# A third accumulator bank in turn, the second batch's first norm in two passes, and a wider spread feed-forward tail in a two-layer transformer kernel

## Chip, cores and metric

The kernel runs on one core of a Trainium2 chip. The metric is the device time of one execution in microseconds. Engines: PE does the matmuls and writes to PSUM, which has eight banks; DVE, ACT and POOL do element-wise work, and POOL doesn't read PSUM here; SP issues every DMA of the program, one after the other. PEld is the weight load ahead of a matmul.

## What is computed

The input x is (2, 1024, 256) in float32. Two layers follow, each attention and then a feed-forward part, and each part is wrapped in a norm before and a norm after ("sandwich"):

```
x = x + ln(attn0(ln(x)))   # 16 heads of 128, weights as FP4 codes x scales, softmax over all 1024 keys
x = x + ln(ffn0(ln(x)))    # silu(gate) * up -> down, ternary weights, inner width 704
x = x + ln(attn1(ln(x)))   # 16 heads of 16, causal
x = x + ln(moe(ln(x)))     # 2 shared + 16 routed experts of 128, top 8 by sigmoid, all computed and weighted

def _layernorm(x, eps=1e-05):
    m = jnp.mean(x, -1, keepdims=True); v = jnp.var(x, -1, keepdims=True)
    return (x - m) / jnp.sqrt(v + eps)
```

## The kernel before

**Numbers.** Activations are split in a high and a low 16-bit part, and products are sums of two or three 16-bit matmuls. So most results that leave PSUM pass ACT (bias, cast to the high part) and then DVE or POOL (the low part, by a subtraction).

**Steps.** `l0_attn` walks through 256 steps, one for each query tile (128 rows) of a head of layer 0. A step issues the scores of its tile (`l0_soft`, into a `pss` buffer), the split of the tile before (`l0_split`, whose transpose goes through SP as `PT`), the product with v for a tile some steps back (`l0_av`, into `psa`), and the jobs that are due: weights of the next pair of heads (`l0_dequant`, into `psy`), q, k and v of the next head (`l0_qk`, `l0_v`, into `psp`), the output product (`l0_out`). Other work is put into steps by `at(step, [functions], spacing)`, with constants at the top of the file: staging of later weights (`PRE`, `FFN_W`), batch 1's first norm (`LN_B`, from step 101), batch 0's feed-forward (`FFN_AT`, steps 120 and 144), its layer-1 q, k, v (`QKV_AT`, 136 and 160) and its layer-1 attention (from step 149), batch 1's first feed-forward half (`FFN1_AT`, 246).

**Tail.** After step 255 a planner in `run` orders what is left against a made-up clock t: `on(t, functions, spacing, cost)` makes work due, `C_FFN`, `C_QKV`, `C_X3`, `C_ROUTE` say when. What is left is the second feed-forward half of batch 1, its layer-1 attention, and nearly all of the experts: 144 units of 12 matmuls (L1233), each followed some units later by its down product of 6 (L1264).

**Order.** PE's order is as the program issues it. The order on DVE, ACT, POOL and SP is made by a list scheduler at build time, from priorities; each engine then works strictly in that order, and an instruction that waits holds up all behind it.

**PSUM.** `pss` has two buffers of two banks; `psp` two of one bank; `psa` and `psy` one bank each. `new_ps` hands out a bank for feed-forward and expert units: `psp`, or in turn with `pss` where layer-1 attention doesn't use it (`l1_over`). The other products take `psp` directly. `psy` serves the dequantization (the last one in step 95) and later the sums of layer-1 attention (`av` in `l1_attn`, L1042).

**Norms.** `stats` (L119, L120) takes mean and variance of two row tiles, `rstd` (L100 to L110) a reciprocal root by eight small dependent DVE instructions on 128x2 values; L147 normalizes, `split` casts on ACT (L219) and subtracts on POOL (L220), and an SP transpose stores the result as `xa` or `xb`. `ln_load` loads two row tiles into `y` (three buffers), normalizes and transposes them; `ln_add` does the norm after a part, the addition, and the next norm.

**Layer-1 q and k.** `l1_qkv.qk` computes 512 columns, `scaled` makes both halves in the tile `l1_sq` (L503 and L506 on ACT, L507 on POOL), three DMAs store it to DRAM (L916) and two load it back in the layout of the attention (L921). For batch 0 `l1_sq` has one buffer (tag `hl_w`); for batch 1 it takes a buffer of the tag `e`, which has three, one of them held by expert weights to the end.

Of the kernel before, what the change touches and what calls it, by code (L numbers as in the profile page):

```python
# [9 lines left out]
F32 = mybir.dt.float32  # L10
# [4 lines left out]
ALU = mybir.AluOpType  # L15
# [32 lines left out]
PAD = 480  # L48
# [8 lines left out]
FFN_W = 102  # L57
LN_B = (101, 105, 103, 106, 115, 120, 117, 121)
# [16 lines left out]
C_FFN = (18.21, 2.02)  # L75
# [3 lines left out]
C_ROUTE = (9.53, 8.0, 30.0, 12.0)  # L79
# [6 lines left out]
class Net:  # L86
# [6 lines left out]
    def rstd(self, var, eps, w):  # L93
# [14 lines left out]
        y = sp.tile([P, NT], F32, name="rs_y")[:, :n]  # L108
# [71 lines left out]

    def ln_start(self, xs):
# [109 lines left out]
    def setup(self, ctx):  # L291
# [19 lines left out]
        self.l1_over = False  # L311
# [95 lines left out]
    def l0_dequant(self, dst, codes, sc, n):  # L407
# [6 lines left out]
        nc.vector.tensor_mul(dst, codes, ps.rearrange("p (k f) -> p k f", k=2))  # L414

# [48 lines left out]
    def l0_qk(self, st, which, c):  # L464
# [6 lines left out]
        ps = self.psp.tile([P, 512], F32, name="psp")  # L471
# [37 lines left out]
    def l0_v(self, st, t4):  # L509
# [4 lines left out]
        ps = self.psp.tile([P, 512], F32, name="psp")  # L514
# [95 lines left out]
    def l0_out(self, st, t2):  # L610
# [6 lines left out]
        ps = self.psp.tile([P, 512], F32, name="psp")  # L617
# [169 lines left out]
    def ffn(self, b, half):  # L787
# [29 lines left out]
        def down(c):  # L817
            ps = self.psp.tile([P, 512], F32, name="psp")
# [58 lines left out]
    def l1_kd(self):  # L877
# [9 lines left out]
        self.n_kd = 0  # L887

    def l1_qkv(self, b, m):
# [4 lines left out]
        def qk(which, c):  # L894
            n = "qk"[which]
            sq = p.tile([P, 2, 512], F16, name="l1_sq", tag=("hl_w", "e")[b], bufs=(1, 3)[b])
# [6 lines left out]
            ps = self.psp.tile([P, 512], F32, name="psp")  # L903
# [29 lines left out]
        def vv(t4):  # L933
# [3 lines left out]
            ps = self.psp.tile([P, 512], F32, name="psp")  # L937
# [18 lines left out]
    def l1_attn(self, b, m, st, yT):  # L956
# [212 lines left out]
    def moe(self, b):  # L1169
# [55 lines left out]
        def unit(c, e):  # L1225
# [15 lines left out]
            nc.vector.scalar_tensor_tensor(th, pu, 1.0 / 16, th, op0=ALU.mult, op1=ALU.mult)  # L1241
# [64 lines left out]
    def run(self):  # L1306
        nc, tc = self.nc, self.tc
        with ExitStack() as ctx:
# [240 lines left out]
```

## Time and profile before

| | us |
|---|---|
| runs: 1808.83, 1806.64, 1804.91; median | 1806.64 |
| the profiled execution's own time | 1804.53 |
| its span, first to last instruction | 1802.8 |
| PE busy (matmuls), DVE, ACT, POOL | 1610.4, 1270.7, 1111.1, 897.7 |
| mean granted PE clock | 0.972 |

The span in stretches. Steps 101 to 121 lie at 405 to 505 us, steps 122 to 158 at 505 to 726 us, step 255 at 1251 us.

| stretch, us | PE busy | DVE busy | ACT busy | POOL busy | granted clock |
|---|---|---|---|---|---|
| 0 to 45 | 22.9 | 25.1 | 21.3 | 17.4 | 1.00 |
| 45 to 405 | 354.1 | 240.5 | 285.3 | 231.5 | 1.00 |
| 405 to 505 | 79.1 | 87.7 | 62.6 | 67.2 | 0.91 |
| 505 to 730 | 190.8 | 169.3 | 139.5 | 127.8 | 0.95 |
| 730 to 1260 | 483.8 | 382.0 | 380.6 | 260.1 | 0.99 |
| 1260 to 1530 | 220.3 | 188.8 | 99.1 | 91.2 | 0.92 |
| 1530 to 1803 | 259.4 | 177.3 | 122.6 | 102.5 | 0.98 |

A row of the timeline reads: start, duration, engine, line, operation, out<-in, shapes, and in brackets the engine's idle time just before and what ended it. PE's busy time counts a matmul longer where the clock is halved, so a busy PE isn't PE at full speed.

### The profile page before, as it was taken

The page shows a single profiled execution, that of the slowest core. Times are in us where ns is not written, and L with a number is a line of the kernel's source. Part 1 is how long each engine was busy: PE and PEld are TensorE (multiplying, and loading weights), DVE is VectorE, ACT ScalarE, POOL GpSimd, SP SyncE. Part 2 cuts the span into 40 slices and gives each one's busy share as a digit, 9 for nine tenths or more (in the row PEclk, how much of TensorE's full clock was granted, in tenths as well). Part 3 has the DMA queues.
Part 4 walks back from the last instruction along what each step waited for, and adds up shares of the span by engine and source line. Part 5 has one row for each costly group of instructions (what it writes and reads, how often), then busy time and mean ns, then how long its engine had stood idle before and what let it go on. Part 6 is the DMA issues. An engine that isn't in the chain of part 4 may idle for free.

```text
span 1802.8 us, 35972 instructions
## 1 busy us (share of the span) xinstructions
PE 1610.4 (89%) x13903; PEld 1074.9 (60%) x13903; DVE 1270.7 (70%) x2559; ACT 1111.1 (62%) x1856; POOL 897.7 (50%) x701
## 2 busy tenths in 40 slices
PE   5999999998789879999989889889867898999998
PEld 2566666665456555565555555555645575777777
DVE  5666666667988769665877677886858578765666
ACT  4788788777566655678667667677333443555432
POOL 3666667556765644445444434475433233333443
PEclk9999999999999999999999999999989899999999
DMA  5886887989966874596566667796753222111120
GB/s 124 205 185 163 170 182 176 230 194 207 243 152 150 152 130 103 107 163 140 132 161 168 190 176 163 184 209 158 238 134 99 75 74 66 46 35 54 59 71 13
DMA packets 634228, 256.19 MB, mean 142 GB/s; under 512 B 574852, under 2 KB 614568, under 8 KB 633800
## 3 DMA queue, kind: packets, MB, share of 16 engines
q1 hardware_dynamic: 634056, 253.88, 60.4%
q8 instruction: 109, 1.79, 0.4%
q14 instruction: 63, 0.52, 0.1%
HBM read 75.61 MB, written 35.33 MB: 62 GB/s over the span
## 4 chain that ended last, share of the span: by engine, by line
PE 48%; DVE 22%; ACT 10%; DMA 8%; issue 6%; POOL 2%; SPq 2%; ACTq 0%; DVEq 0%; POOLq 0%
PE pss L561 10%; PE psa L603 9%; PE psp L1233 7%; DVE nm L565 4%; DVE l_nm L982 3%; PE psp L474 3%; ACT e L567 3%; PE psa L1264 3%; PE psy L1050 3%; ACT hl L575 2%; DMA pre_ew<-hl_w 2%; PE psp L621 2%; SPq L588 2%; PE pss L1023 2%; DVE ln_st L119 1%
## 5 line engine op out<-in xcount | busy, mean ns | idle before, releaser
L576 POOL TENSOR_TENSOR hl<-e,hl 128x1024 f16<-128x1024 f32 x231 | 493.3, 2136 | 422.0 <-ACT hl L575 310.5
L561 PE MATMUL pss<-k,q 128*128 128x512 f16 x1536 | 382.9, 385 | 40.3 <-ACT e L567 10.9
L603 PE MATMUL psa<-PT,v 128*128 128x256 f16 x3072 | 410.8, 275 | 5.4 <-ACT qk L501 5.2
L565 DVE TENSOR_REDUCE nm<-pss 128x1 f32<-128x1024 f32 x256 | 312.4, 1220 | 144.8 <-PE pss L561 144.3
L567 ACT ACTIVATE e<-pss,nm 128x1024 f32<-128x1024 f32 x256 | 285.9, 1117 | 121.2 <-DVE nm L565 103.9
L603 PEld LDWEIGHTS <-v 128*128 128x128 f16 x3072 | 296.1, 99 | 99.1 <-issue 22.0
L575 ACT CAST hl<-e 128x1024 f16<-128x1024 f32 x256 | 268.7, 1050 | 4.4 <-DMA PT<-hl 1.1
L561 PEld LDWEIGHTS <-q 128*128 128x128 f16 x1536 | 146.5, 99 | 190.1 <-issue 47.2
L982 DVE TENSOR_REDUCE l_nm<-pss 128x2 f32<-128x1024 f32 (+3 forms) x152 | 176.1, 1161 | 32.7 <-PE pss L976 28.5
L1233 PEld LDWEIGHTS <-ew 128*128 128x128 f16 x1728 | 167.6, 100 | 49.5 <-issue 24.6
L1250 POOL TENSOR_TENSOR m_h<-m_t,m_h 128x256 f16<-128x256 f32 x144 | 97.3, 678 | 187.2 <-ACT m_h L1249 185.3
L474 PE MATMUL psp<-xa,wr 128*128 128x512 f16 x512 | 131.7, 380 | 13.5 <-DVE k L486 5.2
L1233 PE MATMUL psp<-xa,ew 128*128 128x256 f16 x1008 | 129.5, 280 | 7.4 <-DVE m_t L1241 2.9
L1240 DVE SCALAR_TENSOR_TENSOR m_t<-m_t,psp 128x256 f32<-128x256 f32 x119 | 49.6, 416 | 102.3 <-ACT m_t L1239 99.3
L1249 ACT CAST m_h<-m_t 128x256 f16<-128x256 f32 x144 | 58.1, 404 | 95.6 <-POOL m_t L1248 38.6
L630 DVE SCALAR_TENSOR_TENSOR acc<-psp,r,acc 128x256 f32<-128x256 f32 x240 | 104.2, 475 | 14.8 <-PE psp L621 13.9
L507 POOL TENSOR_TENSOR OT<-qk,OT 128x512 f16<-128x512 f32 x64 | 80.8, 1263 | 55.7 <-ACT OT L506 25.5
L1264 PE MATMUL psa<-ed,m_h 128*128 128x256 f16 x756 | 105.0, 276 | 0.0
L1239 ACT ACTIVATE m_t<-psp 128x256 f32<-128x256 f32 x119 | 45.6, 383 | 87.8 <-PE psp L1233 86.9
L621 PE MATMUL psp<-wo,OT 128*128 128x256 bf16 x512 | 79.5, 277 | 14.6 <-DVE ff_t L813 3.8
L1264 PEld LDWEIGHTS <-m_h 128*128 128x128 f16 x864 | 85.7, 99 | 11.1
L474 PEld LDWEIGHTS <-wr 128*128 128x128 bf16 x512 | 49.0, 98 | 69.4 <-issue 17.4
(186 smaller groups left out, 2631.2 us busy)
## 6 DMA issues: line engine op xcount, KB each, us to landing
cb<-cT_d SPq DMA_DIRECT2D x32, 512.0 KB
w_c<-in_w_codes SPq DMA_DIRECT2D x8, 1024.0 KB
x_d<-y SPq DMA_DIRECT2D x24, 256.0 KB
xr<-x_d SPq DMA_DIRECT2D x24, 256.0 KB
pre_ew<-hl_w SPq DMA_DIRECT2D x18, 256.0 KB
PT<-hl SPq DMA_TRANSPOSE x256
k_d<-k SPq DMA_DIRECT2D x8, 512.0 KB
v_d<-v SPq DMA_DIRECT2D x8, 512.0 KB
```

The source lines that it names most:

```text
L474: nc.tensor.matmul(ps, w()[:, 1 - which, kt, hs], self.xT[0, st["b"], c][:, :, 2 * j + kt, :], start=(kt == 0 and j == 0), stop=(kt == 1 a ...
L561: nc.tensor.matmul(ps[:, sl], q[:, a, qs], k[:, bb, sl], start=(a == 0 and bb == 0), stop=(a == 1), skip_group_check=True)
L565: nc.vector.reduce_max(nm, ps, axis=AX.X, negate=True)
L567: nc.scalar.activation(e, ps, AF.Exp, bias=nm, accum_out=st["sum"][:, qt : qt + 1])
L575: nc.scalar.copy(hl[:, 0, :], e)
L576: (nc.vector if lo_dve else nc.gpsimd).tensor_sub(hl[:, 1, :], e, hl[:, 0, :])
L603: nc.tensor.matmul(ps, v[:, x, kt, :], PT[:, 8 * y + kt, :], start=(kt == 0 and n == 0), stop=(kt == 7 and n == 2))
L621: nc.tensor.matmul(ps[:, 256 * i : 256 * i + 256], OT[:, j, t * P : (t + 1) * P], self.wo[st["p"], h // 2][:, h % 2, :], start=(j == 0), s ...
L630: nc.vector.scalar_tensor_tensor(ys, pv, r, ys, op0=ALU.mult, op1=ALU.add)
L982: nc.vector.reduce_max(nms[t][:, i % 2, :, j0 : j0 + nj, c], pv, axis=AX.X)
L1233: nc.tensor.matmul(ps[:, 256 * o : 256 * o + 256], self.ew[e][:, o, a, kt, :], xT[:, sl, 2 * x + kt, :], start=(n == 0), stop=(n == 5))
L1264: nc.tensor.matmul(py[:, 256 * t : 256 * t + 256], h[:, a, t * P : (t + 1) * P], self.ed[e][:, w, :], start=False, stop=(e == NE - 1 and t ...
```

## The change

1. `new_ps` gives every third request the bank `psy` while `psy_free` is set, and the products that took `psp` directly (q, k, v and output of layer 0, feed-forward down, q, k, v of layer 1) now ask `new_ps`. `psy_free` is set at step 108 if all dequantizations are done, cleared by the first layer-1 sum of a batch, and set again when batch 0's last sum has been copied out. Where `pss` is in turn, it now gets two of six requests, next to each other, and no longer every second one.
2. Batch 1's first norm is split (`ln_ahead`): its four loads and sums are placed at steps 14 to 31, with one `rstd` for all eight tiles; at the steps of `LN_B` the rows are loaded a second time (one step ahead) and only normalized.
3. In the tail the feed-forward's units start at 22.0 and are 3.0 apart on the planner's clock; the norm of the last rows ahead of batch 0's experts (`ln_load(3, 0, 4)` and `(3, 0, 6)`) comes 3.0 later, its DVE instructions behind those of the last expert unit issued; routing comes later.
4. `l1_sq` for batch 0 rotates over three buffers (one of `hl_w`, two of `st`); for batch 1 the k and the q of one column block share one buffer of `e`.
5. A padding tile shrinks by 32 bytes, which the eight kept reciprocal roots take.

The instruction counts of PE, ACT and POOL stay. DVE has 24 fewer (three `rstd` chains), SP four more loads. PE's order is the same up to the tail, but for three places where neighbouring products change sides.

```diff
 RS_S = (3.0 / 8.0) ** 0.2
 RS_START = 1593872682
 RS_NEWTON = 1.66
-PAD = 480
+PAD = 448
 L1_LEAD = 7
 SHIFT_LAG = 2
 AV_LAG = 2
...
 LN_HURRY = 580
 PRE = (12, 2.0, 186, 2.05)
 FFN_W = 102
+LN_A = 14
+PSY_AT = 108
 LN_B = (101, 105, 103, 106, 115, 120, 117, 121)
 L1_W = (100, 104)
 FFN_AT = ((120, 144), 0.55)
...
 MOE_LAG = 6
 MUL_DVE = 0.5
 C_L1 = 3.2
-C_FFN = (18.21, 2.02)
+C_FFN = (22.0, 3.0)
 C_QKV = (6.0, 14.0, 3.4)
 C_ST = (18.0, 26.0)
 C_X3 = 13.09
-C_ROUTE = (9.53, 8.0, 30.0, 12.0)
+C_ROUTE = (18.0, 16.0, 30.0, 16.0)
 C_COST = (1.9, 1.2)
 WS1 = 16.0
 SC1 = 0.5
...
         nc.vector.scalar_tensor_tensor(h, w[:, 0, :], -1.0, w[:, 1, :], op0=ALU.mult, op1=ALU.mult)
         nc.vector.scalar_tensor_tensor(w, h.unsqueeze(1).to_broadcast([P, 2, n]), RS_NEWTON, w, op0=ALU.add, op1=ALU.mult)
         nc.vector.tensor_mul(h, w[:, 0, :], w[:, 1, :])
-        y = sp.tile([P, NT], F32, name="rs_y")[:, :n]
+        y = sp.tile([P, NT], F32, name=keep or "rs_y", **(dict(bufs=1) if keep else {}))[:, :n]
         nc.vector.scalar_tensor_tensor(y, h, -10.0 / 3.0 * RS_S**2, h, op0=ALU.add, op1=ALU.mult)
         nc.vector.scalar_tensor_tensor(y, y, 5.0 * RS_S**4, w[:, 1, :], op0=ALU.add, op1=ALU.mult)
         return y
...
             x = st.pop()
             st.append(self.ln_hl(x, x))
         return [load, norm, lambda: self.ln_T(layer, b, t0, st.pop())]
+    def ln_ahead(self):
+        nc, st = self.nc, {}
+        def load(n):
+            st[n] = self.new_y()
+            with self.gate():
+                nc.sync.dma_start(st[n], self.rows(self.x[0, 1, n // 2], 2 * n % 4, 2))
+        def sums(n):
+            if n == 0:
+                st["mv"] = self.small.tile([P, NT, 2], F32, name="ln_mv8", bufs=1)
+            x = st.pop(n)
+            for i in range(2):
+                t = self.small.tile([P, 6], F32, name="ln_st")
+                nc.vector.bn_stats(t, x[:, i, :])
+                nc.vector.bn_aggr(st["mv"][:, 2 * n + i, :], t)
+            if n == 3:
+                st["r"] = self.rstd(st["mv"][:, :, 1], EPS, NT, "rs_y8")
+        def norm(n):
+            x = st.pop(n)
+            for j in range(2):
+                i = 2 * n + j
+                nc.vector.tensor_scalar(x[:, j, :], x[:, j, :], st["mv"][:, i, 0:1], st["r"][:, i : i + 1],
+                                        op0=ALU.subtract, op1=ALU.mult)
+            hl = st["hl", n] = self.work.tile([P, 4 * D], F16, name="ln_hl", bufs=2)
+            self.split(hl, x, nc.gpsimd)
+        def put(n):
+            self.ln_T(0, 1, 2 * n, st.pop(("hl", n)))
+        return ([(lambda n=n: load(n), lambda n=n: sums(n)) for n in range(4)],
+                [(lambda n=n: load(n), lambda n=n: norm(n), lambda n=n: put(n)) for n in range(4)])
     def ln_start(self, xs):
...
     def new_ps(self):
         self.n_ps += 1
-        if self.l1_over and self.n_ps % 2:
+        if self.psy_free and self.n_ps % 3 == 0:
+            return self.psa.tile([P, 512], F32, name="psy", bufs=1)
+        if self.l1_over and self.n_ps % 3 == 1 + self.n_ps % 2:
             return self.pss.tile([P, T], F32, name="pss")[:, :512]
         return self.psp.tile([P, 512], F32, name="psp")
...
         self.count = {}
         self.n_e1 = 0
         self.n_cb = self.n_ps = 0
-        self.l1_over = False
+        self.l1_over = self.psy_free = False
+        self.n_deq = self.n_lo = 0
         self.qk_todo = []
         self.stored = set()
         self.x = {(0, b, h): self.x_in[b, 512 * h : 512 * h + 512, :] for b in range(B) for h in range(2)}
...
             nc.tensor.matmul(ps[:, 256 * k : 256 * k + 256], self.sel[:, n, k * P : (k + 1) * P],
                              sc, start=True, stop=True)
         nc.vector.tensor_mul(dst, codes, ps.rearrange("p (k f) -> p k f", k=2))
+        self.n_deq += 1
     def l0_weights(self, pair):
...
-        ps = self.psp.tile([P, 512], F32, name="psp")
+        ps = self.new_ps()
...
         def qk(which, c):
             n = "qk"[which]
-            sq = p.tile([P, 2, 512], F16, name="l1_sq", tag=("hl_w", "e")[b], bufs=(1, 3)[b])
+            if b:
+                if which == 1:
+                    st["sq", c] = p.tile([P, 2, 2, 512], F16, name="l1_sqs", tag="e", bufs=3)
+                sq = st["sq", c][:, which, :, :]
+            else:
+                self.n_sq += 1
+                tag, bufs = (("hl_w", 1), ("st", 2), ("st", 2))[self.n_sq % 3]
+                sq = p.tile([P, 2, 512], F16, name="l1_sq", tag=tag, bufs=bufs)
             st[n, c] = p.tile([P, 4, 512], F16, name="l1_" + n, bufs=(L1Q_BUFS, 4)[which])
             if which == 1:
                 d = self.k_d1[self.n_kd % 4]
                 self.n_kd += 1
             else:
                 d = self.dram.tile([2, 50, 4, 512], F16, name="l1_qd", bufs=4)
-            ps = self.psp.tile([P, 512], F32, name="psp")
+            ps = self.new_ps()
             col = which * D + m * P
             k = 0
             for kt in range(2):
...
             es = [live.pop((t, j + d, r)) for d in range(2)]
             if r == 0:
+                self.psy_free = False
                 acc[t] = self.psa.tile([P, 512], F32, name="psy", bufs=1)[:, :256]
                 nc.tensor.matmul(acc[t], self.zero[:, :P], self.zero[:, :256], start=True, stop=False, skip_group_check=True)
             for kb in (2 * r, 2 * r + 1):
...
             if r == t:
                 o = ot[t, j // 2] = p.tile([P, 256], F32, name="l1_o", bufs=2)
                 nc.scalar.copy(o, acc.pop(t))
+                self.n_lo += 1
+                self.psy_free = self.n_lo == 16
                 if j == 2:
                     self.after(FIN_LAG[0], lambda: rows(t))
...
             h = self.work.tile([P, 2, 256], F16, name="m_h", tag="ff_h", bufs=FF_H)
             nc.scalar.activation(th, pg, AF.Tanh, scale=0.5 / WSM)
             nc.vector.scalar_tensor_tensor(th, th, 1.0, pg, op0=ALU.add, op1=ALU.mult)
-            nc.vector.scalar_tensor_tensor(th, pu, 1.0 / 16, th, op0=ALU.mult, op1=ALU.mult)
+            self.m_mark = nc.vector.scalar_tensor_tensor(th, pu, 1.0 / 16, th, op0=ALU.mult, op1=ALU.mult)
             if e < E:
                 cb = st["cb", c, e // 4][:, e % 4, :]
                 k = self.moe_n = self.moe_n + 1
...
             at(FFN_W - 4, [lambda: later[0]()])
             at(FFN_W, self.ffn_weights(), 1)
             at(PRE[2], pre[1], PRE[3])
+            at(PSY_AT, [lambda: setattr(self, "psy_free", self.n_deq == 2 * H0)])
+            ahead = self.ln_ahead()
             for n in range(4):
-                for k, f in zip((0, 0, 1), self.ln_load(0, 1, 2 * n)):
-                    at(LN_B[2 * n + k], [f])
+                for s, f in zip((LN_A + 5 * n, LN_A + 5 * n + 2), ahead[0][n]):
+                    at(s, [f])
+                for s, f in zip((LN_B[2 * n] - 1, LN_B[2 * n], LN_B[2 * n + 1]), ahead[1][n]):
+                    at(s, [f])
             at(L1_W[0], [self.l1_weights])
             at(L1_W[1], [self.l1_bias, self.l1_kd])
             for n in range(2):
...
                 nonlocal routed
                 routed = n
+            def behind(f):
+                with self.tc.issue_after(self.m_mark.ins):
+                    f()
             nxt = {1: 0}
             while True:
                 if not x3 and (3, 0, 6) in self.stored:
...
                     for n in (2, 3):
                         load, norm, put = self.ln_load(3, 0, 2 * n)
                         on(t + C_X3 - 10.0 + 2 * n, [load])
-                        on(t + C_X3 - 4.0 + 2 * n, [norm, put], 1.0)
+                        on(t + C_X3 - 1.0 + 2 * n, [lambda norm=norm: behind(norm), put], 1.0)
                     for c in (2, 3):
                         on(t + C_X3 + C_ROUTE[0] + 2 * (c - 1), [lambda c=c: moe[0]["start"](c)])
                         on(t + C_X3 + C_ROUTE[0] + 2 * (c - 1) + C_ROUTE[1],
```

The two lines that replace a `psp` tile by `new_ps()` occur in `l0_qk`, `l0_v`, `l0_out`, `ffn` (`down`) and `l1_qkv` (`qk` and `vv`).

More of the change, by code (lines that the diff above doesn't have):

```diff
@@ L90, in __init__, with rstd @@
         self.stop = stop
-    def rstd(self, var, eps, w):
+    def rstd(self, var, eps, w, keep=None):
         nc, sp = self.nc, self.small
@@ L616, in l0_out @@
         acc = self.l0_y[st["half"]]
-        ps = self.psp.tile([P, 512], F32, name="psp")
+        ps = self.new_ps()
         for i in range(2):
@@ L817, in down @@
         def down(c):
-            ps = self.psp.tile([P, 512], F32, name="psp")
+            ps = self.new_ps()
             for t in range(2):
@@ L886, in l1_kd @@
                 nc.sync.dma_start(d[g, 48:50, :, :].rearrange("r j t -> (r j) t"), one)
-        self.n_kd = 0
+        self.n_kd = self.n_sq = 0
     def l1_qkv(self, b, m):
@@ L902, in qk @@
                 d = self.dram.tile([2, 50, 4, 512], F16, name="l1_qd", bufs=4)
-            ps = self.psp.tile([P, 512], F32, name="psp")
+            ps = self.new_ps()
             col = which * D + m * P
@@ L936, in vv @@
                 nc.gpsimd.memset(st["v"][:, :, :, 16:17], 1.0)
-            ps = self.psp.tile([P, 512], F32, name="psp")
+            ps = self.new_ps()
             for i in range(4):
```

## Prediction

> **What bounds the kernel now.** First the busy time by stretch, to see where PE, which has most work (1610.4 of 1802.8 us), is not the bound.
>
> ```profile
> 45.00:405.00 360.00, 354.07 (x2627) 231.95 (x2626) 240.47 (x333) 285.29 (x432) 231.54 (x126) 1.00 0.84 188
> 405.00:505.00 100.00, 79.05 (x510) 50.17 (x508) 87.67 (x177) 62.62 (x96) 67.19 (x50) 0.91 1.01 221
> 505.00:730.00 225.00, 190.78 (x1481) 126.75 (x1479) 169.34 (x342) 139.54 (x234) 127.80 (x91) 0.95 0.68 136
> 730.00:1260.00 530.00, 483.76 (x4216) 293.74 (x4213) 382.04 (x617) 380.60 (x595) 260.06 (x155) 0.99 0.70 163
> 1260.00:1530.00 270.00, 220.32 (x2261) 158.78 (x2260) 188.79 (x560) 99.14 (x211) 91.21 (x112) 0.92 0.38 116
> 1530.00:1802.80 272.80, 259.44 (x2699) 202.83 (x2697) 177.32 (x475) 122.63 (x261) 102.53 (x144) 0.98 0.15 46
> ```
>
> The columns after the length are PE, weight load, DVE, ACT, POOL, then granted clock, DMA share and GB/s. PE stands idle 5.9 us in the first row, then 21.0, 34.2, 46.2, 49.7 and 13.4. The second, third and fifth also have the low clock: 0.91 over 100 us, 0.95 over 225 and 0.92 over 270 lack 9, 11 and 22 us of clock, and part of it lies on idle time. The change touches these three. In 730 to 1260 it changes no order that matters: I put it at 0.
>
> Then PE's rows in the timeline with the long waits, and from there the engine that was named, at the same time.
>
> ```profile
> 437.03 0.86 PE L561 MATMUL pss<-k,q 128*128 128x512 f16 x2 [4.41 <-DVE q L481]
> ...
> 638.95 1.87 PE L807 MATMUL psp<-xb,ff 128*128 128x256 f16 x8 [7.74 <-DVE ff_t L813]
> ...
> 1315.39 1.01 PE L908 MATMUL psp<-xb,w 128*128 128x512 f16 x2 [4.95 <-DVE m_t L1241]
> ...
> 1330.12 1.86 PE L807 MATMUL psp<-xb,ff 128*128 128x256 f16 x8 [7.30 <-DVE ff_t L813]
> ...
> 1420.56 0.69 PE L1078 MATMUL psp<-ident,l_y 128*128 128x128 f32 x2 [7.28 <-DVE m_t L1241]
> ```
>
> ```profile
> 430.68 2.06 DVE L105 SCALAR_TENSOR_TENSOR rs_t<-rs_w 128x2 f32<-128x2 f32 x1
> 432.77 2.12 DVE L106 SCALAR_TENSOR_TENSOR rs_w<-rs_t,rs_w 128x4 f32<-128x4 f32 x1
> ...
> 1313.35 0.75 DVE L119 BATCH_NORM_STATS2 ln_st<-y 128x6 f32<-128x256 f32 x2 [5.45 <-DMA y<-x_d]
> ...
> 1328.93 0.75 DVE L119 BATCH_NORM_STATS2 ln_st<-y 128x6 f32<-128x256 f32 x2 [7.09 <-DMA y<-x_d]
> ```
>
> ```profile
> 430.59 4.29 POOL L576 TENSOR_TENSOR hl<-e,hl 128x1024 f16<-128x1024 f32 x2
> ```
>
> ```profile
> 599.91 0.62 ACT L506 CAST l_sq<-qk 128x512 f16<-128x512 f32 x1 [5.51 <-DMA l_kd<-l_sq]
> ...
> 636.93 0.62 ACT L506 CAST l_sq<-qk 128x512 f16<-128x512 f32 x1 [9.59 <-DMA l_kd<-l_sq]
> ...
> 1418.62 0.62 ACT L506 CAST l_sq<-qk 128x512 f16<-128x512 f32 x1 [8.63 <-DMA l_qd<-l_sq]
> ```
>
> So PE's waits go back to three heads of queues. At 428 to 436 the root chain of a batch-1 norm holds DVE: two instructions on 128x2 values take 2.06 and 2.12 us, each just as long as POOL's subtraction beside it. At 594 to 600, 627 to 637 and 1410 to 1418 ACT stands at the cast into `l_sq`, whose buffer waits for its store, with the tanh of the next unit behind it. At 1308 to 1313 and 1322 to 1329 DVE stands at the statistics of rows that are still being loaded.
>
> **Part by part**, against the profiled execution (1804.53 us: span 1802.8 and 1.7 around it; 2.1 below the median of 1806.64).
>
> *Sums in steps 14 to 31 (75 to 141 us).* Added to DVE: 8 statistics of 0.42 and 8 aggregations of 0.17 (their means at 405 to 505) and 8 root instructions at 0.42, the mean there (26.9 us for 64): 8 us. DVE works 240 of 360 us in this stretch, so most of it has cover; but the chain lies between two maxima (L565) for which ACT's exponential and so the score buffer waits. SP gets four loads (1 MB; 5.6 us at the stretch's 188 GB/s) among the transposes; PE's idle total here is 5.9 us although five weight loads made DVE wait 2.4 to 2.9 us, so I count no cost for them. Sum +2; ends 0 (all hidden) and +8 (nothing hidden).
>
> The row of 2.06 us beside POOL says what such an instruction can cost. [...]
>
> *The same norm at steps 101 to 121.* Removed from a DVE that works 87.7 of 100 us: half of 64 root instructions (13.5 us), 8 statistics and 8 aggregations (4.6): 18 us. Kept: eight normalizations (L147), casts, subtractions, transposes. The wait of 2.3 us for the load (DVE at 418.9) goes, as the load is issued a step earlier. PE's waits behind these chains: 4.41; 4.29 at 478.7 (an exponential behind the chains at 464 to 476, one of whose two stays); 2.87 and 1.37 at 493 and 498. I take 4.4 and half of 8.5, 8.7 in all, and a quarter of the missing 9 us of clock: -11. Ends: 0 (the chains that stay, of `ln_add`, take the place) and -20 (all waits and most of the clock).
>
> *Three buffers for `l_sq`, third bank, 505 to 730 us.* ACT loses waits of 5.5 and 9.6 us. PE's waits behind them are 2.81 and 2.14 (at 602 and 607), 7.74 and 1.23: 13.9; I take 11. Late next is the store's way through SP, whose loads (L921) still wait for the landing in the same order. Other waits for a `psp` bank, which a third one can bridge: 3.83 (539), 2.85 (592), 2.07 (676), 1.88 (570): 10.6; half, 5. A bank only defers: where DVE is late, the third fills too. Clock: 3 of the 11 us. Sum -19; ends -4 and -34 (all but nothing of 34.2 us idle stays, or the two casts alone gain).
>
> *Tail, 1260 to 1530 us.* The statistics stand three units later, behind an expert unit: 5.45 and 7.09 us of DVE, 4.95 and 7.30 of PE. The pair buffer leaves two free `e` buffers for two pairs, so the cast at 1418 has no store to wait for: 7.28, and 1.26 behind it. Of 20.8 us I take 15.5. Clock: these waits are the long ones, 6 of 22 us. Against it: at both halves of batch 1 q and k go through DRAM; in the trace from the q product of the first block (ends 1301.5) to its second load (issued 1328.8, about 3 more to land) it takes 30 us, and in PE's new order only about 25 us of matmuls lie between the last q product and the first score, against 46 us that passed before. +3.5. Sum -18; ends +5 (that chain becomes the bound) and -35.
>
> *Last part, 1530 us on.* Units come every 1.97 us; in `psp` pairs a bank returns after two, not four. From the end of a unit's first 12 matmuls its DVE work is done 1.4 us later in a quiet time and 2.5 to 3.3 us where a norm is mixed in (1711 to 1724, 1771 to 1775), where two units apart leave no slack: +1. Between the last projection (L1091) and the routing product (L1182) stand 8 units instead of 11, 15.8 us; the chain of norm, addition, norm and transpose took 16.6 us from 1702.7 to the end of the issue, and must land: +2. Sum +3; ends 0 and +7. The wait of 3.5 us for routing (L1212) stays: those two products are still neighbours.
>
> Total: 2 - 11 - 19 - 18 + 3 = **-43**, so 1761.5 on the profiled execution's scale and **1764** on that of the median.
>
> **Rivals.**
>
> *DVE and POOL stay the bound (1792).* Waits move from one head of a queue to the next: each part but the two casts gains only its lower end or a third: 2 - 4 - 8 - 6 + 3 = -13. For it: DVE is busy 43.2 of 45 us at 450 to 495, two interleaved `ln_add` chains remain there. Against it: elsewhere no engine is above 85%, so waits there are order, not load.
>
> [...]
>
> *Slower, through SP (1815).* In the tail every DMA waits in one queue behind loads that wait for stores. If q's and k's way through DRAM grows from 30 to 40 us, since its stores come behind the loads and transposes moved among them, it outlasts the 25 us of PE's work by 15 at each half, and the low clock after such a wait costs some 5 each: +40, against which the tail's gain of 21.5 (15.5 and 6) stays: +18.5. If the norm at 405 to 505 and the stretch to 730 gain only half, -15 together, then with +2 and +3 the sum is +8.5: 1815. It decides from some 32 us of such waits and clock on (21.5 + 15 - 5); if those two parts gain all that I forecast, from 46.5. For it: SP's own waits at L921 (8.9 us) and L223 (7.9 us) between 1270 and 1400. Against: only 0.4 us of PE's waits in the tail names a DMA.
>
> **How the numbers follow.** Less than 0.2% (3.6 us) from the median is what a measurement of this kernel can't tell from no change. The forecast's case (1741 to 1785) has 0.58, everything returns (below) 0.10, DVE stays the bound (1785 to 1803) 0.18, no difference 0.04, slower 0.10. So faster 0.86. The range 1732 to 1802 leaves out some 0.05 below and 0.14 above.
>
> **What would show it.** Right: at 400 to 500 us DVE's busy share falls by some 15 us and only `ln_add` root chains stay; no ACT row `l_sq` ends a wait on `l_kd` or `l_qd`; the waits on `y<-x_d` in the tail are gone; clock in the three stretches near 0.97; PE's wait rows name `psy` as well. Wrong: new PE waits on `l_q` or `l_k` loads, on `xb<-ln_hl` or `xa<-ln_hl`, or the old waits under another line. A root chain of over 8 us at 135 to 145 us would make the first part's cost wrong.

## The result and the profile after

The changed kernel takes 1827.71 us (median; 1823.99 to 1831.95) where the kernel before takes 1807.67: 1.0114 times as long, 95% interval 1.0083 to 1.0144. It is slower by 1.1%; the forecast was 1764 and faster. Its profiled execution took 1830.72 us, with a span of 1829.0, 26.2 above that of before.

The busy time by stretch of the kernel after (columns as before: PE, weight load, DVE, ACT, POOL, granted clock, DMA share, GB/s):

```profile
45.00:405.00 360.00, 350.65 (x2577) 228.30 (x2576) 244.14 (x351) 282.81 (x428) 228.81 (x125) 1.00 0.84 188
405.00:505.00 100.00, 81.95 (x560) 53.28 (x559) 70.09 (x132) 64.16 (x98) 65.67 (x52) 0.95 1.02 217
505.00:730.00 225.00, 195.08 (x1517) 129.28 (x1518) 173.66 (x352) 142.27 (x240) 132.24 (x94) 0.95 0.74 145
730.00:1260.00 530.00, 480.58 (x4179) 291.95 (x4175) 383.14 (x611) 378.84 (x590) 259.07 (x155) 0.99 0.70 162
1260.00:1530.00 270.00, 202.29 (x2040) 149.02 (x2039) 164.98 (x508) 90.72 (x195) 82.90 (x104) 0.88 0.36 107
1530.00:1829.00 299.00, 279.97 (x2926) 216.20 (x2924) 201.43 (x529) 132.52 (x277) 110.56 (x154) 0.97 0.16 50
```

PE's idle time is 9.4 us from 45 to 405 (5.9 before), then 18.1 (21.0), 29.9 (34.2), 49.4 (46.2) and, from 1260 to 1530, 67.7 (49.7), there at a clock of 0.88 (0.92). So two of the three stretches lost 3 and 4 us of idle time where I had forecast 8.7 and 16 us (the rest of the 11 and 19 was clock). The tail has 18 us more of it, and by its lower clock lacks 11 us more (0.88 for 0.92 over 270 us).

PE's rows in the timeline of after with its long waits:

```profile
456.76 1.46 PE L603 MATMUL pss<-k,q 128*128 128x512 f16 x6 [2.65 <-DMA k<-k_d]
474.31 2.29 PE L603 MATMUL pss<-k,q 128*128 128x512 f16 x5 [5.24 <-DMA k<-k_d]
...
1316.49 1.87 PE L849 MATMUL psp<-xb,ff 128*128 128x256 f16 x8 [5.50 <-DMA xb<-ln_hl]
...
1342.95 2.29 PE L1285 MATMUL psy<-xa,ew 128*128 128x256 f16 x10 [8.89 <-DVE ff_t L855]
...
1472.64 1.19 PE L1072 MATMUL pss<-l_q,l_k 50*128 50x256 f16 x8 [24.93 <-DMA l_q<-l_sT]
```

The waits behind DVE's root chains (4.41 at 437 and others) are gone, and PE waits for loads of k in their place. In the tail one wait of 24.93 us has come: PE's scores need the shift rows of q (`l_sT`), and those come through SP. SP's rows in the timeline of after tell why:

```profile
1421.95 2.67 SPq L965 DMA_DIRECT2D l_kd<-l_sqs  x3
1432.92 0.68 SPq L970 DMA_DIRECT2D l_k<-l_kd  x2
1433.70 3.57 SPq L965 DMA_DIRECT2D l_qd<-l_sqs  x3
1445.20 0.78 SPq L970 DMA_DIRECT2D l_q<-l_qd  x2
1446.03 2.50 SPq L965 DMA_DIRECT2D l_kd<-l_sqs  x3
1456.80 0.66 SPq L970 DMA_DIRECT2D l_k<-l_kd  x2
1457.50 3.20 SPq L965 DMA_DIRECT2D l_qd<-l_sqs  x3
1468.86 1.00 SPq L970 DMA_DIRECT2D l_q<-l_qd  x2
1469.91 1.34 SPq L1058 DMA_DIRECT2D l_q<-l_sT  x2
```

A store of three transfers, then the load that waits for them to land, four times over: 11 us from a store's first issue to its load, 12 to the next store, 48 from the first store to the shift rows. Those had been ready since the cast of `l_sT` at 1441.74, but stand behind two more round trips. The first store and the shift rows of the same four trips in before:

```profile
1395.59 1.84 SPq L916 DMA_DIRECT2D l_kd<-l_sq  x3
...
1446.84 1.34 SPq L1009 DMA_DIRECT2D l_q<-l_sT  x2
```

There PE came to the first of these scores (eight products in a row) at 1454.7: 59 us after the first store, with some 5 us to spare. In after the trips began at 1422.0 and PE was there at 1447.7, after 26 us. The chain takes about as long (48 us, 51 in before); what covers it has shrunk.

To see where each kernel gains or loses, I compare when PE begins the scores of a step, and a row of output projections (L1091 in before) in the tail. The numbers are us behind the profile of before (minus: ahead), each from one profiled execution:

| kernel | step 34 | 36 | 104 | 121 | 158 | 255 | 5th projection | 6th | end |
|---|---|---|---|---|---|---|---|---|---|
| after | +1.5 | +6.4 | +8.7 | +0.5 | -4.0 | +0.8 | -3.7 | +29.7 | +26.2 |
| after, FFN 2.02 apart | +1.0 | +5.8 | +9.3 | -0.8 | -7.1 | -2.4 | -5.5 | -5.5 | -3.5 |
| before, FFN 3.0 apart | +0.6 | +0.6 | +0.6 | -0.6 | +2.5 | +7.6 | +4.0 | +39.4 | +32.6 |
| after, no third bank | +2.1 | +6.9 | +11.9 | +4.7 | -0.2 | +8.3 | +3.9 | +37.9 | +33.4 |
| after, old store buffers | -0.2 | +4.9 | +11.4 | +2.1 | +6.3 | +15.8 | +10.3 | +45.1 | +41.6 |
| after, norm as before (pad 480) | +0.5 | +0.5 | +0.6 | -2.5 | -12.4 | -7.7 | -14.8 | +19.0 | +14.9 |
| after, roots held | +1.9 | +1.9 | +5.5 | -4.0 | -10.0 | -2.7 | -7.2 | +26.4 | +23.0 |
| after, stores in two pieces | +2.0 | +6.8 | +8.7 | -1.0 | -14.1 | -9.3 | -33.2 | -24.8 | -28.3 |
| before, stores in two pieces | -0.1 | -0.1 | -0.3 | -1.3 | -11.1 | -10.4 | -31.8 | -31.8 | -33.0 |

How far such a number can be trusted is seen in the third row: PE's order there is that of before through step 255, and it is still 2.5 us off at step 158 and 7.6 at step 255. The jump between the 5th and the 6th projection is far beyond that, and the step of 4.8 to 5.1 between steps 34 and 36 is either there, in five of these kernels, or not at all.

### The profile page after: what moved, and what is told of

The parts are those of the page before. It is cut to its first block, busy times and chain, and to the rows that moved or that the text cites. A ratio compares the mean times of both kernels' runs of the same rounds, so it can differ in the third digit from the quotient of the medians.

```text
span 1829.0 us, 35926 instructions
## 1 busy us (share of the span) xinstructions
PE 1613.9 (88%) x13903; PEld 1078.5 (59%) x13903; DVE 1261.4 (69%) x2535; ACT 1111.4 (61%) x1856; POOL 895.6 (49%) x701
## 4 chain that ended last, share of the span: by engine, by line
PE 31%; DVE 18%; ACT 7%; DMA 7%; issue 5%; POOL 2%; SPq 1%; ACTq 0%; POOLq 0%; DVEq 0%
PE psp L1285 7%; PE pss L603 4%; PE psa L645 3%; DVE l_nm L1031 3%; PE psa L1316 3%; PE psy L1100 3%; DVE nm L607 2%; ACT e L609 2%; PE pss L1072 2%; DMA pre_ew<-hl_w 2%; DMA PT<-hl 1%; DVE ln_st L121 1%; ACT hl L617 1%; PE psp L516 1%; PE psp L865 1%
## 5 line engine op out<-in xcount | busy, mean ns | idle before, releaser
L645 PE MATMUL psa<-PT,v 128*128 128x256 f16 x3072 | 410.4, 275 | 12.4 <-ACT qk L543 11.6
L516 PE MATMUL psp<-xa,wr 128*128 128x512 f16 x480 | 126.4, 387 | 8.6 <-DVE k L528 3.4
L672 DVE SCALAR_TENSOR_TENSOR acc<-psp,r,acc 128x256 f32<-128x256 f32 x226 | 98.1, 474 | 17.0 <-PE psp L663 16.4
L1084 ACT ACTIVATE e1x<-pss 128x1024 f32<-128x1024 f32 (+1 forms) x80 | 75.0, 940 | 47.6 <-PE pss L1072 37.8
L1072 PE MATMUL pss<-l_q,l_k 50*128 50x256 f16 (+1 forms) x640 | 65.8, 265 | 33.2 <-DMA l_q<-l_sT 24.9
```

The costliest lines, as they stand in the source:

```text
L516: nc.tensor.matmul(ps, w()[:, 1 - which, kt, hs], self.xT[0, st["b"], c][:, :, 2 * j + kt, :], start=(kt == 0 and j == 0), stop=(kt == 1 a ...
L645: nc.tensor.matmul(ps, v[:, x, kt, :], PT[:, 8 * y + kt, :], start=(kt == 0 and n == 0), stop=(kt == 7 and n == 2))
L672: nc.vector.scalar_tensor_tensor(ys, pv, r, ys, op0=ALU.mult, op1=ALU.add)
L1072: nc.tensor.matmul(ps[:, 512 * g + o : 512 * g + o + n], st["k", kb // 4][rows, j, (kb % 4) * P : (kb % 4 + 1) * P], st["q", t // 2][rows, ...
```

## Experiments

Theory at the start: the later feed-forward units in the tail shrink what covers q's and k's way through SP; the early sums cost at step 34. Rivals: the routing, or the buffers that let projections run ahead, make the long wait.

**Feed-forward units as close as before.**

```diff
-C_FFN = (22.0, 3.0)
+C_FFN = (18.21, 2.02)
```

> The kernel after, with the feed-forward units of the tail due at 18.21 and 2.02 apart again (22.0 and 3.0 after); all else of the change stays. Theory: the later feed-forward units put the second q/k projections of batch 1 so late that the four store-and-load round trips in SP's queue (11.5 us each) are no longer covered, and PE stands 24.9 us at the scores that need the shift rows. Then this wait falls below 8 us and the time to 1796 to 1808. Rival: the wait comes from the later routing and norm, or from the pair buffer that lets the projections run ahead; then it stays above 18 us and the time within 5 us of 1828.

1803.03 us, 0.9971 of before (0.9953 to 0.9988). The long wait is gone; what is left on SP's chain, in PE's rows of the timeline:

```profile
1312.71 1.89 PE L849 MATMUL pss<-xb,ff 128*128 128x256 f16 x8 [10.25 <-DMA xb<-ln_hl]
1348.31 0.49 PE L1234 MATMUL psp<-rg,xa 128*128 128x16 f16 x12 [4.35 <-DMA xa<-ln_hl]
1416.85 0.76 PE L1072 MATMUL pss<-l_q,l_k 50*128 50x256 f16 x4 [8.88 <-DMA l_q<-l_sT]
```

This one constant (the units' start and spacing) is worth 25 us, the whole loss and a little more. The wait that I expected below 8 is 8.88. All three rows name a DMA, where before's long waits in the tail named DVE.

**All of the tail's due times as before.**

```diff
-C_FFN = (22.0, 3.0)
+C_FFN = (18.21, 2.02)
...
-C_ROUTE = (18.0, 16.0, 30.0, 16.0)
+C_ROUTE = (9.53, 8.0, 30.0, 12.0)
...
-                        on(t + C_X3 - 1.0 + 2 * n, [lambda norm=norm: behind(norm), put], 1.0)
+                        on(t + C_X3 - 4.0 + 2 * n, [norm, put], 1.0)
```

> The kernel after, with the tail's three due times as before: feed-forward units at 18.21 and 2.02 apart, routing at 9.53 and 8.0 later (12.0 for batch 1), the norm of the third layer at its old time and without the wait for the expert unit. The early sums, the third bank and the buffers of the split q and k stay. Theory (the feed-forward spacing alone makes the wait): within 6 us of the kernel with only the spacing undone. Rival (routing and norm make it): at least 12 us faster than that kernel.

1807.57 us, 0.9992 of before (0.9980 to 1.0004): 4.5 us behind the kernel above. Routing and the later norm did not make the wait; they are worth some 4 us, if anything.

**The spacing alone, in the kernel before.** Only `C_FFN = (22.0, 3.0)`.

> The kernel before with one edit, feed-forward units of the tail due at 22.0 and 3.0 apart (18.21 and 2.02 before). Theory: this number alone makes the long wait, so PE stands 15 to 30 us at scores that need the shift rows of q between 1400 and 1480 us, and the time is 15 to 32 us above before. Rival: it does so only together with the buffers that let the projections run ahead or with the later routing; then it is within 8 us of before.

1837.10 us, 1.0129 of before (1.0078 to 1.0180). PE's rows in the timeline:

```profile
1454.82 0.40 PE L1023 MATMUL pss<-l_q,l_k 50*128 50x256 f16 x2 [6.82 <-ACT e L1035]
...
1480.94 1.20 PE L1023 MATMUL pss<-l_q,l_k 50*128 50x256 f16 x8 [16.86 <-DMA l_q<-l_sT]
```

The wait for the shift rows is there without any of the other edits, 16.86 us of it: the spacing makes it by itself. The 6.82 us ahead of it come by another way, through an exponential on ACT. Before has a wait that goes back to ACT too (7.28 at 1420, in the prediction's rows, where a cast into `l_sq` waits 8.63 us for its store). I take this one for the same, an estimate from those rows, and not for the spacing's work.

**The third bank taken away.** `psy_free` is never set.

```diff
-                self.psy_free = self.n_lo == 16
...
-            at(PSY_AT, [lambda: setattr(self, "psy_free", self.n_deq == 2 * H0)])
```

> The kernel after without the third bank in turn; the other changes stay. Theory: a bank only defers a wait, so by step 158 it stands within 4 us of the kernel after, and the end within 6 us of 1828. Rival, as the prediction had it: the bank takes 5 us or more out of 505 to 730 us, and this kernel is slower than the one after by as much before the tail.

1834.89 us, 1.0144 of before (1.0125 to 1.0164), 7 us above after; in the table it is 3.8 behind after at step 158 and 7.5 at step 255. Neither wins cleanly: 3.8 is just within the theory's 4, the end is outside its 6, and 7.5 at step 255 is what one profile scatters. And of the 3.8 us, 3.2 were there at step 104 (11.9 for 8.7), ahead of step 108, where the bank first comes in. So these runs don't show what the bank is worth up to step 158; the two kernels' intervals for the whole time overlap.

**Batch 1's first norm as before**, loads, sums and roots at steps 101 to 121.

```diff
-            ahead = self.ln_ahead()
             for n in range(4):
-                for s, f in zip((LN_A + 5 * n, LN_A + 5 * n + 2), ahead[0][n]):
-                    at(s, [f])
-                for s, f in zip((LN_B[2 * n] - 1, LN_B[2 * n], LN_B[2 * n + 1]), ahead[1][n]):
-                    at(s, [f])
+                for k, f in zip((0, 0, 1), self.ln_load(0, 1, 2 * n)):
+                    at(LN_B[2 * n + k], [f])
```

> The kernel after with batch 1's first norm as before: loads, sums and root chains at steps 101 to 121, none in steps 14 to 31. Theory: the sums cost 4.8 us where PE waits at step 34 (a root instruction of 2.1 us ahead of a maximum) and give back some 9 between steps 108 and 121, so this kernel is 5 us ahead of the one after at step 36 and about 4 us behind it at step 121; end 1829 to 1836. Rival: the new waits of 2.6, 5.2 and 2.1 us on loads of k at 454 to 491 us come from the four loads one step earlier and their place in the queue; then they are gone here and it is level or ahead at step 121.

1848.54 us, 1.0221 of before (1.0204 to 1.0239): worse than after by 21, which neither theory had. It was already 7.5 us behind before at step 20, ahead of all that the edit puts in. Leaving out the early norm also leaves out the eight kept roots, 32 bytes, which the smaller pad makes room for; so every tile of the work pool lay 32 bytes lower (in the built program PT starts at 41952 instead of 41984). Hence the next run.

**The same, with the pad back at 480.** Its instruction order is that of the run above.

```diff
-PAD = 448
+PAD = 480
```

> The last kernel (batch 1's first norm as before) with the pad at the head of the constants at 480 bytes instead of 448, so that all tiles of the work pool lie at the addresses that they have before and after; the order of all instructions is the same as without it. In the last run they all lay 32 bytes lower, and the DMA share was 0.80 at 159 GB/s from 940 to 1000 us where after had 0.72 at 184. Theory: the 20 us that it lost against after come mostly from that address; now 1826 to 1836, DMA share per GB/s as after, and the early sums themselves are worth +4 to -4. Rival: the loss is that of the norm's old place; then it stays at 1843 to 1850.

1819.87 us, 1.0057 of before (1.0031 to 1.0082). The busy time by stretch, first at 448, then at 480 bytes:

```profile
45.00:405.00 360.00, 349.02 (x2553) 226.82 (x2552) 235.20 (x327) 280.70 (x425) 226.59 (x123) 1.00 0.94 185
```

```profile
45.00:405.00 360.00, 353.36 (x2622) 231.29 (x2620) 240.35 (x333) 285.22 (x431) 231.32 (x126) 1.00 0.84 188
```

0.94 of the DMA engines' time moves 185 GB/s, and 0.84 moves 188: 14% more time per byte for tiles 32 bytes off, and 28.7 us in the whole (1.6% by the two ratios). How the address costs the time no run shows. The loss that I had laid at the norm's old place was the address. Against this kernel the change's early norm loses 8 us, by intervals that only just part (up to 1.0082, and from 1.0083).

From its PE rows:

```profile
437.71 1.03 PE L603 MATMUL pss<-k,q 128*128 128x512 f16 x2 [4.42 <-DVE q L523]
...
460.56 2.72 PE L603 MATMUL pss<-k,q 128*128 128x512 f16 x6 [2.97 <-ACT e L609]
```

The old waits behind the root chains are there again and the waits on k are gone. The move traded one set for the other: 10 us of k against 11.3 of the chains (4.42, 2.97 and 3.90). The DMA share of that stretch is 1.01 in before and 1.02 in after, so its loads can hardly have slack; that those of k come late for this reason was not tried apart.

**The roots put off to step 101.**

```diff
-            if n == 3:
-                st["r"] = self.rstd(st["mv"][:, :, 1], EPS, NT, "rs_y8")
         def norm(n):
             x = st.pop(n)
+            if n == 0:
+                st["r"] = self.rstd(st["mv"][:, :, 1], EPS, NT, "rs_y8")
```

> The kernel after with the eight root instructions of the early norm moved from step 31 to step 101, ahead of the first normalization; loads and sums stay in steps 14 to 31. Theory: the 4.9 us between steps 34 and 36 are root instructions of 1.7 and 2.1 us beside POOL's subtraction ahead of a maximum; so that loss goes (step 36 is 1 to 2 us behind before, not 6.4) and part of it returns at step 101: end 1823 to 1829. Rival: it is the loads or the sums; then step 36 stays 5 to 7 us behind before.

1835.76 us, 1.0157 of before (1.0112 to 1.0202), and still 5.0 us lost between steps 34 and 36. But the trace shows the roots at 145 to 151 us, as in after: the scheduler orders DVE's instructions by what is ready, and the step at which one is written down does not hold it. The run says nothing on the cause.

**The roots held there**, queued behind the maximum of step 100.

```diff
-            if n == 3:
-                st["r"] = self.rstd(st["mv"][:, :, 1], EPS, NT, "rs_y8")
         def norm(n):
             x = st.pop(n)
+            if n == 0:
+                with self.tc.issue_after(self.top.ins):
+                    st["r"] = self.rstd(st["mv"][:, :, 1], EPS, NT, "rs_y8")
...
-            nc.vector.reduce_max(nm, ps, axis=AX.X, negate=True)
+            self.top = nc.vector.reduce_max(nm, ps, axis=AX.X, negate=True)
```

> The kernel after with the eight root instructions put off to step 101 and, unlike in the last kernel, held there: they are queued on VectorE behind the maximum of step 100. (In the last kernel they still ran at 145 to 151 us, since an engine's order goes by what is ready.) Theory: root instructions of 1.7 and 2.1 us beside POOL's subtraction, ahead of a maximum, are the 4.9 us lost between steps 34 and 36; then step 36 is 1 to 2 us behind before, and 2 to 4 of the 4.9 stay won at step 121; end 1822 to 1828. Rival: it is TensorE's own order, which the early items change by one swap of neighbours at steps 31 to 35; then step 36 stays 5 to 7 us behind before.

Step 36 is 1.9 us behind, as step 34 is: the loss is gone, with TensorE's order as in after. It was the roots. The timeline of after shows how:

```profile
146.43 2.13 POOL L618 TENSOR_TENSOR hl<-e,hl 128x1024 f16<-128x1024 f32 x1 [2.46 <-ACT hl L617]
146.91 1.67 DVE L107 SCALAR_TENSOR_TENSOR rs_t<-rs_w 128x8 f32<-128x8 f32 x1
...
149.44 2.13 POOL L618 TENSOR_TENSOR hl<-e,hl 128x1024 f16<-128x1024 f32 x1 [0.88 <-POOL hl L618]
149.49 2.10 DVE L109 TENSOR_TENSOR rs_t<-rs_w 128x8 f32<-128x8 f32 x1
...
151.91 2.35 DVE L607 TENSOR_REDUCE nm<-pss 128x1 f32<-128x1024 f32 x2
153.22 1.11 ACT L609 ACTIVATE e<-pss,nm 128x1024 f32<-128x1024 f32 x1 [3.91 <-DVE nm L607]
...
154.96 1.44 PE L645 MATMUL psa<-PT,v 128*128 128x256 f16 x6 [3.22 <-ACT qk L543]
```

Two of the eight end only with POOL's subtraction beside them, a maximum stands behind them, ACT's exponential behind that, and ACT's emptying of `psa`, which PE needs, behind that. At step 101 two of the held roots took 2.00 and 2.07 us again, and step 104 is 5.5 behind; at step 121 the kernel is 4.5 us ahead of after. Of the whole time I can't say so much: 1831.49 us, 1.0120 of before (1.0083 to 1.0157), no different from after, though its profiled execution has a span 3.2 shorter.

**The old buffers for the split q and k.**

```diff
-            if b:
-                if which == 1:
-                    st["sq", c] = p.tile([P, 2, 2, 512], F16, name="l1_sqs", tag="e", bufs=3)
-                sq = st["sq", c][:, which, :, :]
-            else:
-                self.n_sq += 1
-                tag, bufs = (("hl_w", 1), ("st", 2), ("st", 2))[self.n_sq % 3]
-                sq = p.tile([P, 2, 512], F16, name="l1_sq", tag=tag, bufs=bufs)
+            sq = p.tile([P, 2, 512], F16, name="l1_sq", tag=("hl_w", "e")[b], bufs=(1, 3)[b])
```

> The kernel after with the buffers for the split q and k as before (one for batch 0, three single ones for batch 1). Theory: the buffers are worth 6 to 14 us between steps 136 and 158 (casts that wait for a store come back with 5 to 10 us each), and nothing in the tail, where the wait is in SP's queue: the wait of 24.9 us stays above 15 and the end is 1832 to 1842. Rival: the buffers, by letting four projections run ahead, are what makes the long wait; then it falls below 10 us and the end is at or under 1822.

1841.21 us, 1.0172 of before (1.0135 to 1.0209), 13.5 above after. ACT's rows in the timeline:

```profile
606.63 0.62 ACT L548 CAST l_sq<-qk 128x512 f16<-128x512 f32 x1 [6.46 <-DMA l_kd<-l_sq]
...
643.14 0.62 ACT L548 CAST l_sq<-qk 128x512 f16<-128x512 f32 x1 [12.22 <-DMA l_kd<-l_sq]
```

The waits for the store are back, and step 158 comes 10.3 us later than in after. In the tail PE waits 6.73 us (behind an exponential on ACT) and 16.48 (for the shift rows): the buffers don't make the long wait. With them no cast there waits for a store, and all of it falls on the shift rows.

**Stores in two pieces, in the kernel after.** This takes the chain itself. A store wrote to both halves of the DRAM tile with one transfer per part; now one transfer per half.

```diff
-                    nc.sync.dma_start(d[:, 16 * i : 16 * i + 16, :, :].rearrange("g r j t -> g (r j) t"), sq[:, a, :])
+                    for g in range(2):
+                        nc.sync.dma_start(d[g, 16 * i : 16 * i + 16, :, :].rearrange("r j t -> (r j) t"), sq[64 * g : 64 * g + 64, a, :])
```

> The kernel after, with each store of the split q and k (layer 1) issued as two, one for each half of the partitions, so that each writes one piece of 64 rows of 1 KB. In after the four stores of three transfers move 48 GB/s while nothing else moves and each waits 11.5 us from its first issue to the load behind it. Theory: the queue's round trip is bytes at a low rate; two pieces are spread over more of the DMA engines, the round trip falls to 6 to 9 us and PE's wait of 24.9 us by 10 to 20; time 1805 to 1818. Rival: the trip is latency and issue time; then it stays at 11 us or grows by the three more issues (0.5 us each) and the time stays within 6 us of 1828.

1779.45 us, 0.9827 of before (0.9770 to 0.9884): 48 us less than after, more than the theory's most. First two rows by stretch from after, each between a store's last issue and the load behind it, then one of this kernel across three stores and the loads between them:

```profile
1424.70:1432.90 8.20, 8.00 (x108) 5.45 (x104) 3.10 (x5) 6.74 (x11) 1.83 (x2) 1.00 0.14 46
1436.50:1445.20 8.70, 8.70 (x117) 6.85 (x114) 6.48 (x24) 4.40 (x9) 2.81 (x3) 1.00 0.13 45
```

```profile
1399.00:1413.00 14.00, 13.80 (x177) 9.05 (x169) 7.59 (x21) 8.56 (x15) 3.67 (x4) 1.00 0.50 132
```

A DMA share of 0.13 to 0.14 is about what two of the sixteen engines would make if they alone were busy (0.125): an estimate from the share, as these rows don't show the engines one by one. The old store's DRAM side is 2 by 64 by 512, that of a piece 64 by 512. With the pieces the share is 0.50, more than two engines can make, at 132 GB/s instead of 45 and 46. How the shape sets the share isn't shown. SP's rows in the timeline, and PE's at the scores:

```profile
1398.11 4.35 SPq L966 DMA_DIRECT2D l_qd<-l_sqs  x6
1404.18 0.79 SPq L971 DMA_DIRECT2D l_q<-l_qd  x2
1405.01 3.65 SPq L966 DMA_DIRECT2D l_kd<-l_sqs  x6
1408.77 4.79 SPq L966 DMA_DIRECT2D l_qd<-l_sqs  x6
1413.60 0.90 SPq L971 DMA_DIRECT2D l_k<-l_kd  x2
1414.66 0.77 SPq L971 DMA_DIRECT2D l_q<-l_qd  x2
1415.48 1.40 SPq L1059 DMA_DIRECT2D l_q<-l_sT  x2
...
1419.30 0.78 PE L1073 MATMUL pss<-l_q,l_k 50*128 50x256 f16 x8 [1.10 <-DMA l_q<-l_sT]
```

The four trips, begun at 1392.4, take 23 us to the shift rows instead of 48, most of it issue, and the scores wait 1.1 us. Where a load stands right behind its store, it now comes 1.0 and 1.7 us after the store's last issue ends, for 7.9 to 8.3 in after. The stretch 1260 to 1530 idles 31.5 us on PE (after 67.7), with no single wait above 3.5 us, and 505 to 730 has 23.1 (after 29.9).

**Both: two apart, and stores in two pieces.**

> The kernel after with the feed-forward units due at 18.21 and 2.02 apart again, and with the stores in two pieces. Theory: what is left of PE's waits on q's way (8.9 us at 1408 and 10.3 at 1302 in the run with the spacing alone) falls by half, 1790 to 1799, below both kernels. Rival (round trip is latency): 1800 to 1806, as with the spacing alone.

1772.68 us, 0.9781 of before (0.9734 to 0.9829). Below what the theory allowed. With short trips the spacing is worth 7 us instead of 25.

**The pieces alone, in the kernel before.**

> The kernel before with one edit, each store of the split q and k in two pieces of 64 rows. Theory: the stores are the head of ACT's and SP's queues already in before (casts that wait 5.5, 9.6 and 8.6 us for a store), so the pieces alone are worth 14 (those PE waits at 602, 607, 635 and 1413 us with their clock, half) to 30 us: 1778 to 1795. Rival: they help only where the later feed-forward units or the deeper buffers put the chain on the path; then within 6 us of before.

1772.06 us, 0.9795 of before (0.9770 to 0.9819): 38 us from one line, more than the 30 I had set as the most. ACT's wait of 9.6 us at the cast is gone and that of 5.5 has become 1.1, without one more buffer; the stretch 1260 to 1530 idles 33.0 us on PE:

```profile
1260.00:1530.00 270.00, 237.03 (x2504) 173.19 (x2504) 201.29 (x583) 112.61 (x237) 98.87 (x124) 0.95 0.36 109
```

**What is left of the change beside it**: two apart, pieces, norm as before (pad 480).

> The kernel after with the feed-forward units at 18.21 and 2.02 apart, stores in two pieces, and batch 1's first norm as before (pad at 480): what is left of the change is the third bank, the buffers of the split q and k, and the later routing and norm of the tail. Theory: the early sums cost 8 us net, so this is 1761 to 1768, 5 to 11 under the kernel with them. Rival: with the stores out of the way the norm's old root chains come back onto the path; then within 4 us of 1773.

1766.40 us, 0.9762 of before (0.9727 to 0.9797), the lowest of all; 6 us under the kernel with the early norm, as the theory has it, but the intervals overlap, with this and with the pieces alone. Once the stores are fast, the third bank, the buffers and the later routing together are worth 0.3%, which these intervals don't tell from nothing.

## Why the prediction was wrong

*Tail: forecast -18, came out at +29 (from step 255 to the 6th projection).* This is the step that failed, and its term is "q and k go through DRAM ... it takes 30 us ... against 46 us that passed before. +3.5". I had timed the way of one block in the first half. In the second half k and q go through SP twice each, each load waiting for its store before the next store is issued: four trips, 12 us each and 48 in all, with the shift rows at the end; and PE's cover there fell from 59 to 26 us. 48 and 3 to land, less 26, is the 25 that PE waited. In the term's own measure, from the last q product on: the way took 37.5 us for the 30, and 12.6 us passed on PE for the 25 (45.5 in before, as the term has it). So both sides of the term were wrong. The spacing alone made the wait, in before's surroundings too. The 6 us of clock that the tail was to gain became a loss of 11. Most of it lies in the wait of 24.93 us itself, where the clock is 0.58 and PE has no work; behind it the clock is 0.53 for 3.4 us (1472.6 to 1476.0) and then 1.00, some 1.6 us of clock by these two numbers, where the rival through SP put some 5 on a wait of 15.

Of the tail's old waits I took 15.5 us. The one behind the cast at 1418 went, but those on the norm's statistics did not: DVE still stood 9.94 us for `y<-x_d` at 1338, PE 8.89 behind it and 5.50 for `xb<-ln_hl`. Even with the spacing undone the stretch idles 48.9 us on PE against 49.7. With the stores in pieces, in the kernel after, none of these waits is left: what goes through SP there had stood behind the same slow stores, and the instructions that I read as heads of queues were behind another one. The rival "slower, through SP" had the place and the mechanism, with 15 us at each half where it was 25 at the second; I gave it 0.10, since little of PE's waiting in before named a DMA. But the row that spoke was there: SP's own waits, and ACT's casts that waited 5.5 to 9.6 us for a store of 384 KB. I took the store's time as given and never divided bytes by time: a store of 384 KB takes some 8 us from its last issue on, at some 46 GB/s. The row by stretch of before for such a time:

```profile
1398.00:1406.00 8.00, 8.00 (x115) 5.16 (x115) 6.07 (x11) 4.89 (x9) 1.83 (x2) 1.00 0.14 46
```

*Sums in steps 14 to 31: +2, measured +4.9.* The mechanism (a root beside POOL's subtraction, ahead of a maximum) was named, and the range held it; I took the mean over rows, where the two long roots both fell on the path. Two of the eight met a subtraction.

*The norm at steps 101 to 121: -11, measured -3* (from step 36 to 121 after gains 5.9 us, the kernel with the old norm 3.0). The chains went and loads of k took their place. With the early sums, -9 was forecast for the whole move, and it costs 8. The line of this stretch in the prediction reads DMA share 1.01; I used it for DVE and PE and not for the loads.

*Three buffers and the third bank, 505 to 730: -19, of which single runs give 10.3 for the buffers and nothing sure for the bank* (11 and 5 taken, and 3 of clock). The buffers' mechanism and size were about right. The bank's 5 is neither shown nor refuted, and the clock is 0.95 as it was. In the table after gains only 4.5 from step 121 to 158, and the kernel with the old norm 9.9; what took the rest wasn't settled.

*730 to 1260: 0, measured +5*, within what one profile scatters. *Last part: +3, measured -3.5* from the 6th projection on; nothing rests on it.

*The pad* was in the change and not in the prediction. There it keeps all addresses in place and costs nothing; taken alone (28.7 us) it would have weighed as much as the tail (29). A slip in the sums: the total of the rival with DVE and POOL as the bound (1792) is on the profiled execution's scale and that of the one through SP (1815) on the median's, 2.1 us apart. And the low clock isn't only found at the longest waits: in before it is 0.50 behind waits of 3.83 (540 to 543 us) and 3.46 us (1729 to 1733) too.

## To carry to other kernels

Before a wait on a transfer is covered with buffers or moved, divide its bytes by its time and look at the DMA share beside it: here 0.13 to 0.14 at 44 to 46 GB/s, while SP's queue stood still, went with the shape of a store, and the one line that changed it was worth more (38 us in before) than all the reordering. A chain through an in-order queue is measured end to end, all its round trips, against the work that lies between its first store and its last user; work taken out of that gap comes back as a wait (here 26 us of work for 59, and a wait of 24.93). An edit that adds or drops a small tile moves the addresses of all behind it (32 bytes made 28.7 us here), so keep them fixed when comparing.

## What was not expected of the hardware

- Stores whose DRAM side has an outer dimension of 2 moved 44 to 46 GB/s at a DMA share of 0.13 to 0.14; with the stores in pieces of 64 rows, a stretch of three of them and the loads between moved 132 GB/s at 0.50.
- Work tiles 32 bytes off made each byte take 14% more DMA time (0.94 at 185 GB/s against 0.84 at 188) and the kernel 28.7 us longer.
- DVE's root instructions on the eight tiles' values took 0.16 to 0.17 us in after with POOL idle, and 1.67 and 2.10 beside POOL's subtraction of 2.13 (146.91 and 149.49 us). In the kernel with the roots held, two of the eight took 2.00 and 2.07 us at step 101 and the others 0.15 to 0.18.
